# Sorted feed-forward: first eight tiles from the counts of 12 and 15 token tiles

## Chip, cores and metric

The kernel runs on one core of one Trainium2 chip. The metric is the device time of one execution in microseconds; of several executions the median is given.

## What is computed

Two perceiver layers over 64 sequences of 32 latents with 256 features, float32 throughout: 2048 rows, 16 token tiles of 128. Each layer adds a cross-attention, a self-attention and a feed-forward to `x`, each on a layer norm. The change touches the end of the second layer, its self-attention and its feed-forward with one expert of eight for each row:

```python
def _L1_ffn_ref(hidden_states, router_w, gate_w, up_w, down_w):
    H, I, E = (256, 512, 8)
    x = hidden_states.reshape(-1, hidden_shape[-1])
    route = jax.nn.sigmoid(x @ router_w)
    max_ind = jnp.argmax(route, axis=1)
    max_prob = jnp.take_along_axis(route, max_ind[:, None], axis=1)
    out = jnp.zeros_like(x)
    for e in range(num_experts):
        mask = (max_ind == e)[:, None]
        h = jax.nn.silu(x @ gate_w[e]) * (x @ up_w[e])
        out = out + jnp.where(mask, h @ down_w[e], 0.0)
    out = out * max_prob
    return out.reshape(hidden_shape)

x = x + _L1_attn_ref(_layernorm(x, axis=-1), ...)
x = x + _L1_ffn_ref(_layernorm(x, axis=-1), ...)
```

## The kernel before, in words

TensorE (PE) multiplies, VectorE (DVE) and ScalarE (ACT) do the element-wise work, GpSimd (POOL) does some of it and issues the indirect transfers (scatters), and SyncE (SP) issues the other transfers.

**Second self-attention (lines 1556 to 1844).** A loop of slots, `t` from 0 to 16. In slot t TensorE makes the scores of tile t+1 (`score`, line 294), the weighted values of tile t-1 (`gather`, 1627), the values of tile t+1 (1602) and the transposed probabilities of tile t (`heads_on_partitions`, 263). DVE scales the scores and takes their maximum (245, 254), POOL subtracts it (255), ACT takes the exponential (1594). After `gather` DVE divides (1635, 1637) and POOL adds the result to the residual `x` (1640). In the slots before 12 the features of the next group of four tiles are made too (1249), and their norms (`norm`, 205). Weights of one expert matrix after another are loaded by SP in slots 0 to 11 (1519). PE, DVE and ACT keep the order in which the code is written (`manual_schedule`); POOL and SP get theirs from a scheduler.

**Router.** For each group of token tiles: `route_stats` (mean and variance of the finished rows, DVE 161, 162), `route_norm` (reciprocal root on POOL 148, 149; scale and shift on DVE 1657, 1658; normalised rows on ACT 1664; the two numbers kept in the row on POOL 1668), `route_turn` (transposes 1678, copies 1681), `route` (logits 1690, sigmoid from an exponential on ACT 1699, one-hot of the best expert on DVE 1700 to 1708, running counts `cum` 1712), and `send` (rank within the expert by two matmuls 1720 and 1723, slot number on DVE 1727 to 1733, then one scatter a token tile on POOL, 1736). A scatter writes 128 rows of `x`, with probability, token index, scale and shift behind them, to places in a DRAM buffer `srt`, which has a region of 2048 rows for each expert. Groups of four tiles, 0 to 11, take these steps in slots 4g+5, 4g+6, 4g+7 and 4g+8; tiles 12 to 14 and tile 15 take theirs in slots 15, 16 and after the loop.

**Table.** `count` (1746 to 1773) sums the one-hots of all 16 tiles, gets from them how many tiles of 128 rows each expert needs, and makes for the 23 tiles of the sorted feed-forward the first row in `srt` (`rowi`) and the offset of the expert's weights (`tei`).

**Sorted feed-forward (1851 to 1941).** 23 tiles, since eight experts that are each rounded up to whole tiles need at most 16+7. `fetch_rows` loads the rows of a tile by SP (1860), waiting for all scatters (`sent`), normalises them (DVE 1864), keeps the token index `ti` (1868, four buffers) and transposes them (PE 1871, ACT copy 1873). In the loop over j TensorE does the gate product of tile j (1879), the transposes of tile j-1's hidden rows (1891, DVE copy 1893), the up product of tile j, the transposes of tile j+1's rows and the down product of tile j-1 (1899). ACT does Silu (1934), DVE the product with up (1935) and the scaled output with the residual (1907), POOL scatters it to `out` (1910). Only PE keeps a written order here.

Of the kernel before, what the change touches and what calls it, by code (L numbers as in the profile page):

```python
# [45 lines left out]
def perceiver_kernel(ctx: ExitStack, tc: tile.TileContext, a: dict, out: bass.AP):  # L46
# [158 lines left out]
    def norm(g, part, name, mvs, lat):  # L205

        if g >= NG:
            return
        two = range(2 * (part % 2), 2 * (part % 2) + 2)
        if part == 0:  # L210
            mvs[g], lat[g] = sm(f"lnm_{name}{g}", [P, 4, 2]), []
        if part < 2:
            for i in two:
                stats(mvs[g][:, i, :], xs[4 * g + i], f"{name}{g}_{i}")
        else:
            lat[g] += [ln_out(xs[4 * g + i], *mvs[g], i, f"{name}{g}") for i in two]
        if part == 1:
            mvs[g] = ln_scale(mvs[g], f"{name}{g}", power=True)
# [1322 lines left out]
    ntile = numbers("ntile", [[P, NS]], 0, NS)  # L1541
# [6 lines left out]
    nc.vector.memset(cum[:, 0, :], 0.0)  # L1548
    slots = w1.tile([P, NT], mybir.dt.uint32, name="slots")
    for t in range(NT):  # L1550
        nc.gpsimd.tensor_copy(xf[t][:, D : D + 1], token[:, t : t + 1])

# [3 lines left out]
    with tc.tile_pool(name="wE", bufs=2) as work, tc.tile_pool(  # L1556
# [85 lines left out]
        rows = {}  # L1642
        sent = []

        def route_stats(t):
            g, i = divmod(t, 4)
            if i == 0:
                rows[g] = sm(f"lnf_{g}", [P, 4, 2])
            stats(rows[g][:, i, :], xs[t], f"f{t}")

        def route_norm(ts):
            g, i0 = divmod(ts[0], 4)
            n_ = len(ts)
            mv = rows[g][:, i0 : i0 + n_, :]
            sc2 = sm(f"lnq_f{ts[0]}", [P, 4, 2])
            rs = rstd_of(mv, n_, f"f{ts[0]}", True)
            nc.vector.tensor_copy(sc2[:, :n_, 0], rs)
            nc.vector.scalar_tensor_tensor(
                sc2[:, :n_, 1], mv[:, :, 0], -1.0, rs, ALU.mult, ALU.mult
            )  # L1660
            rows[ts] = []
            for i, t in enumerate(ts):
                y = xnp.tile([P, D], F32, tag="xn", name=f"xn_f{t}")
                nc.scalar.activation(
                    y, xs[t], AF.Identity, scale=sc2[:, i, 0:1], bias=sc2[:, i, 1:2]
                )
                rows[ts].append(y)
                nc.gpsimd.tensor_copy(xf[t][:, D + 2 : DP], sc2[:, i, :])

        def route_turn(ts, k):  # L1670
            if k == 0:
                rows[ts] = rows[ts], work.tile(
                    [P, KC, 512], F32, tag="xTf", name=f"xTf{ts[0]}", bufs=1
                )
            xn, xT = rows[ts]
            tp = ps2.tile([P, 512], F32, tag="mm", name=f"tpf{ts[0]}_{k}")
            for i in range(len(ts)):
                nc.tensor.transpose(
                    tp[:, i * P : (i + 1) * P], xn[i][:, k * P : (k + 1) * P], ident
                )  # L1680
            nc.scalar.copy(xT[:, k, : len(ts) * P], tp[:, : len(ts) * P])

        def route(ts):

            n_, t0 = len(ts), ts[0]
            xT = rows.pop(ts)[1]
            l_ps = ps2.tile([P, n_, NE], F32, tag="mm", name=f"lpf{t0}")
            for i in range(n_):
                for k in range(KC):
                    nc.tensor.matmul(  # L1690
                        l_ps[:, i, :],
                        xT[:, k, i * P : (i + 1) * P],
                        f_r[:, k, :],
                        start=(k == 0),
                        stop=(k == KC - 1),
                    )
            rt = sm(f"rtf_{t0}", [P, n_, NE])

            nc.scalar.activation(rt, l_ps, AF.Exp, scale=-1.0)
            nc.vector.tensor_scalar_add(rt, rt, 1.0)  # L1700
            nc.vector.reciprocal(rt, rt)
            mx = sm(f"mxf_{t0}", [P, n_])
            nc.vector.tensor_reduce(mx, rt, AX.X, ALU.max)
            nc.vector.tensor_tensor(rt, rt, bc(mx, 2, NE), ALU.is_equal)
            nc.vector.tensor_tensor(rt, rt, bc(desc[:, 0:NE], 1, n_), ALU.mult)
            m2 = sm(f"m2f_{t0}", [P, n_])
            nc.vector.tensor_reduce(m2, rt, AX.X, ALU.max)
            nc.vector.tensor_tensor(
                oh[:, t0 : t0 + n_, :], rt, bc(m2, 2, NE), ALU.is_equal
            )  # L1710
            for i, t in enumerate(ts):
                nc.vector.tensor_add(cum[:, t + 1, :], cum[:, t, :], oh[:, t, :])
                nc.gpsimd.tensor_copy(xf[t][:, D + 1 : D + 2], mx[:, i : i + 1])

        def send(ts):

            n_ = len(ts)
            gs = slice(ts[0], ts[0] + n_)
            rank = ps2.tile([P, n_ * NE], F32, tag="mm", name=f"rank{ts[0]}")
            nc.tensor.matmul(  # L1720
                rank, tri, oh[:, gs, :].rearrange("p t e -> p (t e)"), start=True, stop=False
            )
            nc.tensor.matmul(
                rank, one, cum[:, gs, :].rearrange("p t e -> p (t e)"), start=False, stop=True
            )
            sl = sm(f"slr_{ts[0]}", [P, n_, NE])
            nc.vector.tensor_tensor(
                sl, rank.rearrange("p (t e) -> p t e", e=NE), bc(base, 1, n_), ALU.add
            )
            nc.vector.tensor_tensor(sl, sl, oh[:, gs, :], ALU.mult)  # L1730
            slf = sm(f"slf_{ts[0]}", [P, n_])
            nc.vector.tensor_reduce(slf, sl, AX.X, ALU.add)
            nc.vector.tensor_copy(slots[:, gs], slf)
            for t in ts:

                d = nc.gpsimd.indirect_dma_start(
                    out=srt,
                    out_offset=bass.IndirectOffsetOnAxis(ap=slots[:, t : t + 1], axis=0),
                    in_=xf[t],
                    in_offset=None,  # L1740
                ).ins
                for e in sent:
                    tc.declare_no_dep(d, e.name, reason="rows of different tokens")
                sent.append(d)

        def count():

            cnt = ps2.tile([P, NE], F32, tag="mm", name="cnt")
            nc.tensor.matmul(cnt, one, cum[:, NT, :], start=True, stop=True)
            n_t = w1.tile([P, NE, NT], F32, name="n_t")  # L1750
            nc.vector.tensor_tensor(n_t, bc(cnt, 2, NT), bc(n128, 1, NE), ALU.is_gt)
            tiles = w1.tile([P, NE], F32, name="tiles")
            nc.vector.tensor_reduce(tiles, n_t, AX.X, ALU.add)
            nc.vector.tensor_scalar_mul(tiles, tiles, float(P))
            last = w1.tile([P, NE], F32, name="last")
            nc.vector.tensor_tensor_scan(last, one[:, 0:NE], tiles, 0.0, ALU.mult, ALU.add)

            L = NE - 1
            te = w1.tile([P, NS, L], F32, name="te")
            nc.vector.tensor_tensor(te, bc(ntile, 2, L), bc(last[:, 0:L], 1, NS), ALU.is_ge)  # L1760
            tef = w1.tile([P, NS], F32, name="tef")
            nc.vector.tensor_reduce(tef, te, AX.X, ALU.add)
            nc.vector.tensor_tensor(te, te, bc(tiles[:, 0:L], 1, NS), ALU.mult)
            row = w1.tile([P, NS], F32, name="row")
            nc.vector.tensor_reduce(row, te, AX.X, ALU.add)
            nc.vector.tensor_sub(row, ntile, row)
            nc.vector.scalar_tensor_tensor(row, tef, float(B * S), row, ALU.mult, ALU.add)
            rowi = w1.tile([P, NS], I32, name="rowi")
            nc.vector.tensor_copy(rowi, row)
            nc.vector.tensor_scalar_mul(tef, tef, float(FE))  # L1770
            tei = w1.tile([P, NS], I32, name="tei")
            nc.vector.tensor_copy(tei, tef)
            return rowi, tei


        routing = {}
        for g in range(3):
            for z, step in enumerate((route_norm, route_turn, route, send)):
                routing[4 * g + 5 + z] = [(step, tuple(range(4 * g, 4 * g + 4)))]
        most, rest = (12, 13, 14), (15,)  # L1780
        routing[15].append((route_norm, most))
        routing[16] += [(route_turn, most), (route_norm, rest)]
        routing[17] = [
            (route, most), (route_turn, rest), (send, most), (route, rest), (send, rest)
        ]

        def router_parts(t):

# [246 lines left out]
```

## Time and profile before

| | us |
|---|---|
| median of 5 runs | 1287.35 (1277.8 to 1293.15) |
| the profiled execution | 1289.4 |
| its span | 1287.6 |
| PE, DVE, ACT, POOL busy | 1186.9, 773.2, 554.5, 367.2 |
| first matmul of the sorted feed-forward | 1143.14 after the span's start |
| last matmul | 1279.75, 1.99 long |

A row of the timeline has start, duration, engine, line, operation, what is written and read, the number of instructions taken together, and in brackets how long the engine had been idle and what ended that. PEld is the weight load of TensorE. A row of busy times by stretch has the stretch, its length, busy time with number of instructions for PE, PEld, DVE, ACT and POOL, the granted TensorE clock as a share of full speed, the mean share of busy transfer engines, and GB/s. DMA_INDIRECT on POOL is a scatter; the duration is POOL's, not the transfer's.

### The profile page before, as it was taken

The page shows a single profiled execution, that of the slowest core. Times are in us where ns is not written, and L with a number is a line of the kernel's source. Part 1 is how long each engine was busy: PE and PEld are TensorE (multiplying, and loading weights), DVE is VectorE, ACT ScalarE, POOL GpSimd, SP SyncE. Part 2 cuts the span into 40 slices and gives each one's busy share as a digit, 9 for nine tenths or more (in the row PEclk, how much of TensorE's full clock was granted, in tenths as well). Part 3 has the DMA queues.
Part 4 walks back from the last instruction along what each step waited for, and adds up shares of the span by engine and source line. Part 5 has one row for each costly group of instructions (what it writes and reads, how often), then busy time and mean ns, then how long its engine had stood idle before and what let it go on. Part 6 is the DMA issues. An engine that isn't in the chain of part 4 may idle for free. (4 is left out here: it accounts for less than half of the span.)

```text
span 1287.6 us, 26074 instructions
## 1 busy us (share of the span) xinstructions
PE 1186.9 (92%) x10173; PEld 831.2 (65%) x10173; DVE 773.2 (60%) x1801; ACT 554.5 (43%) x1297; POOL 367.2 (29%) x438
## 2 busy tenths in 40 slices
PE   7999999999999998999889999999998798669997
PEld 4556767677776565776757766767765566536664
DVE  5676147778768775433297878776774564434343
ACT  2437344464543641213355656565563454311111
POOL 2333334445442621000154252010011354411111
PEclk8889999999999998979989999999999797669999
DMA  5021122333242423902253353111100344011110
GB/s 151 34 69 35 28 75 75 122 117 108 76 140 67 150 74 123 260 4 68 56 159 103 63 149 96 46 36 46 36 1 2 133 150 150 18 38 42 43 40 18
DMA packets 94971, 103.08 MB, mean 80 GB/s; under 512 B 37792, under 2 KB 71329, under 8 KB 94626
## 3 DMA queue, kind: packets, MB, share of 16 engines
q1 hardware_dynamic: 92978, 97.19, 25.7%
q0 software_dynamic: 1872, 4.23, 0.9%
q8 instruction: 81, 1.33, 0.4%
q14 instruction: 40, 0.33, 0.1%
HBM read 69.45 MB, written 32.85 MB: 79 GB/s over the span
## 5 line engine op out<-in xcount | busy, mean ns | idle before, releaser
L1348 ACT ACTIVATE pp<-Sd,nm 128x257 f32<-128x257 f32 x256 | 118.0, 474 | 77.9 <-DVE nm L1344 73.3
L761 PE MATMUL qb<-xT_b,b_q 128*128 128x256 f32 x512 | 123.4, 389 | 0.0
L761 PEld LDWEIGHTS qb<-xT_b,b_q 128*128 128x128 f32 x512 | 96.4, 193 | 39.9 <-issue 19.8
L852 PE MATMUL yb<-b_o,oTb 128*128 128x256 f32 x512 | 115.1, 384 | 0.0
L852 PEld LDWEIGHTS yb<-b_o,oTb 128*128 128x128 f32 x512 | 97.6, 192 | 14.0 <-issue 1.0
L1357 DVE TENSOR_TENSOR pp<-pp,rd 128x514 f32<-128x514 f32 x128 | 102.3, 799 | 2.1
L1344 DVE TENSOR_REDUCE nm<-Sd 128x2 f32<-128x514 f32 x128 | 83.0, 685 | 19.3 <-PE Sd L1336 19.2
L1379 ACT COPY pTd<-pt 128x512 f32<-128x512 f32 x112 | 61.5, 599 | 53.6 <-PE pt L1373 53.6
L1396 PE MATMUL od<-pTd,na 128*64 128x256 f32 x480 | 67.0, 401 | 12.9 <-issue 11.6
L780 POOL TENSOR_TENSOR q2b<-qTb 128x512 f32<-128x512 f32 x64 | 65.5, 1052 | 28.2 <-ACT qTb L769 17.0
L1336 PE MATMUL Sd<-ct,qTd 64*128 64x257 f32 x480 | 68.9, 404 | 0.3 <-ACT pp L1348 0.2
L769 ACT COPY qTb<-qb 128x512 f32<-128x512 f32 x64 | 37.4, 584 | 72.4 <-PE qb L761 70.8
L1373 PE MATMUL pt<-cst,pp 128*128 128x128 f32 x512 | 66.9, 274 | 0.0
L871 POOL TENSOR_TENSOR ynb<-ynb,vec 128x256 f32<-128x256 f32 x16 | 11.6, 724 | 188.3 <-DVE ynb L870 188.3
L1373 PEld LDWEIGHTS pt<-cst,pp 128*128 128x128 f32 x512 | 58.9, 141 | 9.8 <-issue 5.4
L1134 PE MATMUL qd<-xT_d,d_m 128*128 128x256 f32 x256 | 64.4, 395 | 0.2 <-ACT xT_d L230 0.2
L814 DVE RECIPROCAL rqb<-rqb 128x512 f32<-128x512 f32 x16 | 53.5, 3344 | 17.8 <-ACT rqb L809 17.8
L643 PE MATMUL yc<-c,hc 128*128 128x256 f32 x256 | 59.9, 390 | 2.6 <-DVE hc L638 2.6
L1412 PE MATMUL yd<-d_n,co 128*128 128x256 f32 x256 | 62.3, 398 | 0.0
L1910 POOL DMA_INDIRECT out_dram<-os,ti x23 | 22.6, 984 | 126.0 <-DVE os L1907 103.1
L1134 PEld LDWEIGHTS qd<-xT_d,d_m 128*128 128x128 f32 x256 | 46.8, 192 | 17.0 <-issue 6.4
L1412 PEld LDWEIGHTS yd<-d_n,co 128*128 128x128 f32 x256 | 49.3, 198 | 13.1 <-issue 6.5
(371 smaller groups left out, 2381.5 us busy)
## 6 DMA issues: line engine op xcount, KB each, us to landing
srt<-pad SPq DMA_DIRECT2D x17, 1040.0 KB
mb<-maskd SPq DMA_DIRECT2D x64, 128.0 KB
ct<-ctd SPq DMA_DIRECT2D x30, 257.0 KB
rct<-in_ctxT_dram SPq DMA_DIRECT2D x32, 128.5 KB
rrt<-in_ctxT_dram SPq DMA_DIRECT2D x64, 64.2 KB
ctd<-rct SPq DMA_DIRECT2D x32, 128.5 KB
nad<-rna SPq DMA_DIRECT2D x16, 256.0 KB
fw<-in_f_wg_dram SPq DMA_DIRECT2D x8, 512.0 KB
```

What stands on the lines that cost most here:

```text
L761: nc.tensor.matmul(q_ps[:, hh, :], b_q[:, k, h * P : (h + 1) * P], xT[:, k, c0 : c0 + 256], start=(k == 0), stop=(k == KC - 1),)
L780: nc.gpsimd.tensor_tensor(q2[:, 4 * h4 : 4 * h4 + 4, :], q, q, ALU.mult)
L852: nc.tensor.matmul(y_ps, oT[:, h, :], b_o[:, h, :], start=(h == 0), stop=(h == NH - 1))
L1134: nc.tensor.matmul(q_ps[:, r, :], m[:, k, pr * P : (pr + 1) * P], xT[:, k, c0 : c0 + 256], start=(k == 0), stop=(k == KC - 1),)
L1336: nc.tensor.matmul(s_ps[:, hh, :NKV], qT[hs, b % 8, 4 * u : 4 * u + 4, :], ct[hs, b % 4, :], start=True, stop=True,)
L1344: nc.vector.tensor_reduce(nm, s_ps[:, :, :NKV], AX.X, ALU.max, negate=True)
L1348: nc.scalar.activation(pp[:, hh, :], s_ps[:, hh, :NKV], AF.Exp, bias=nm[:, hh : hh + 1], accum_out=sd[:, hh : hh + 1],)
L1357: nc.vector.tensor_tensor(pp, pp, bc(rd, 2, NKV), ALU.mult)
L1373: nc.tensor.transpose(pt[:, hh * 256 + u * P : hh * 256 + u * P + P], probs[b][:, u, hh, c * P : (c + 1) * P], ident,)
L1379: nc.scalar.copy(pT[:, c, :], pt)
L1396: nc.tensor.matmul(o_ps[64 * hh : 64 * hh + 64, 0, :], na[:, j, c, :], pT[:, c, hh * 256 : (hh + 1) * 256], start=(c == 0), stop=(c == 1),)
L1412: nc.tensor.matmul(y_ps, co[:, pr, :], n[:, pr, :], start=(pr == 0), stop=False)
```

## The change

1. `count` becomes `give_out(n_tok, n)`, called three times. After 12 token tiles it gives out 5 tiles, after 15 three more, after 16 the last 15. The first two times it counts only full tiles (`n128e`, whole multiples of 128 rows); what has been given out is kept in `done`, and the later tables begin behind it.
2. The steps of groups 0 to 11 come a slot sooner. `send` is split into `places` (rank and slot number of a group) and `send(t)` (one scatter), and the scatters are spread: one in each of slots 8 to 11, two in slots 12 and 13, four in slot 14.
3. The counts of 12 tiles are taken in slot 15. The first five row loads come right behind the slots, and the router of tiles 12 to 14 and of 15, their scatters, and the second and third table lie between the steps of tiles 0 to 2 of the sorted feed-forward, with logits and counts in the PSUM buffers of tag "y".
4. The sorted feed-forward writes out the order of DVE and ACT too. Row loads are up to five tiles ahead (eight buffers), norms of rows two.
5. In `route_norm` the scale and shift are made by POOL and no longer by DVE; in `norm` the shift is made one part later.

```diff
         else:
+            if part == 2:
+                mv, rs = mvs[g]
+                sh = sm(f"lnh_{name}{g}", [P, 4])
+                nc.vector.scalar_tensor_tensor(sh, mv[:, :, 0], -1.0, rs, ALU.mult, ALU.mult)
+                mvs[g] = rs, sh
...
+    n128e = numbers("n128e", [[P, NT]], 0, NT)
+    nc.vector.tensor_scalar_add(n128e, n128e, float(P - 1))
...
     def route_norm(ts):
...
-            nc.vector.tensor_copy(sc2[:, :n_, 0], rs)
-            nc.vector.scalar_tensor_tensor(
-                sc2[:, :n_, 1], mv[:, :, 0], -1.0, rs, ALU.mult, ALU.mult
-            )
+        nc.gpsimd.tensor_copy(sc2[:, :n_, 0], rs)
+        nc.gpsimd.tensor_tensor(rs, rs, mv[:, :, 0], ALU.mult)
+        nc.gpsimd.tensor_scalar(sc2[:, :n_, 1], rs, -1.0, None, ALU.mult)
...
+    def send(t):
+        nc.vector.tensor_copy(slots[:, t : t + 1], place.pop(t))
+        d = nc.gpsimd.indirect_dma_start(
...
+        for e in sent + loads:
+            tc.declare_no_dep(d, e.name, reason="rows of different tokens")
+        sent.append(d)
+
+    def give_out(n_tok, n, ps, tag):
+        last = n_tok == NT
+        cnt = ps.tile([P, NE], F32, tag=tag, name=f"cnt{n_tok}")
+        nc.tensor.matmul(cnt, one, cum[:, n_tok, :], start=True, stop=True)
+        yield
+        n_t = w1.tile([P, NE, NT], F32, tag="n_t", name=f"n_t{n_tok}")
+        nc.vector.tensor_tensor(
+            n_t, bc(cnt, 2, NT), bc(n128 if last else n128e, 1, NE), ALU.is_gt
+        )
+        left = w1.tile([P, NE], F32, tag="left", name=f"left{n_tok}")
+        nc.vector.tensor_reduce(left, n_t, AX.X, ALU.add)
+        if n_tok > 12:
+            nc.vector.tensor_sub(left, left, done)
...
+        if not last:
+            nc.vector.tensor_scalar(upto, upto, float(n), 0.0, ALU.subtract, ALU.max)
+            nc.vector.tensor_sub(left, left, upto)
+            nc.vector.tensor_scalar_max(left, left, 0.0)
+            nc.vector.tensor_add(done, done, left)
+        yield rowi, tei
...
+            g, z = divmod(t - 5, 4)
+            ts = tuple(range(4 * g, 4 * g + 4))
             fns = []
+            if 0 <= g < 3:
+                if z == 0:
+                    fns += [lambda k=k: route_turn(ts, k, work, ps2, "mm") for k in range(KC)]
+                if z == 1:
+                    fns.append(lambda: route(ts, ps2, "mm"))
+                if z == (1 if g == 2 else 2):
+                    fns.append(lambda: places(ts, ps2, "mm"))
             return fns
+
+        sends = {8: (0,), 9: (1,), 10: (2,), 11: (3,), 12: (4, 5), 13: (6, 7), 14: (8, 9, 10, 11)}
...
+            if t == NT - 1:
+                given = give_out(12, 5, ps2, "mm")
+                parts.append(lambda: next(given))
...
+            if t == NT - 1:
+                table = {0: next(given)}
             if t >= NT - 1:
                 route_stats(t - 1)
+                route_norm(most if t < NT else rest)
...
             if 0 < t < NT - 1:
                 route_stats(t - 1)
+                if t % 4 == 0:
+                    route_norm(tuple(range(t - 4, t)))
+            for t_ in sends.get(t, ()):
+                send(t_)
...
+            for j in range(5):
+                load_rows(j)
+            for k in range(KC):
+                route_turn(most, k, work, ps2, "y")
+            for j in range(2):
+                rows_norm(j)
+            rows_turn(0)
+
+            def router(n_):
+                if n_ == 0:
+                    route(most, ps2, "y")
+                elif n_ == 1:
+                    for k in range(KC):
+                        route_turn(rest, k, work, ps2, "y")
+                elif n_ == 2:
+                    places(most, ps2, "y")
+                    for t in most:
+                        send(t)
+                elif n_ == 3:
+                    given = give_out(15, 3, ps2, "y")
+                    next(given)
+                    table[5] = next(given)
+                    for j in range(5, 8):
+                        load_rows(j)
+                elif n_ == 4:
+                    route(rest, ps2, "y")
+                elif n_ == 5:
+                    places(rest, ps2, "y")
+                    send(rest[0])
+                elif n_ == 6:
+                    given = give_out(NT, NS - 8, ps2, "y")
+                    next(given)
+                    table[8] = next(given)
...
                     g_ps = gate_up(j, 0, rows_of[j][2], off)
+                if j == 0:
+                    router(0)
...
+                router(2 * j + 1)
                 if j + 1 < NS:
-                    rows_of[j + 1] = fetch_rows(j + 1)
+                    rows_turn(j + 1)
                 if j > 0:
                     r, ti, _ = rows_of.pop(j - 1)
                     down(j - 1, r, ti, *made.pop(j - 1))
+                if j < 3:
+                    router(2 * j + 2)
+                if 3 <= j and j + 5 < NS:
+                    load_rows(j + 5)
+                if j + 2 < NS:
+                    rows_norm(j + 2)
```

## The prediction

> **What bounds the kernel now.** I read the page first, then busy time by stages, then the timeline of the stage where TensorE falls idle. On the page TensorE is busy 92% of the span, and its row and the clock row dip together in one place:
>
> ```profile
> PE   7999999999999998999889999999998798669997
> PEclk8889999999999998979989999999999797669999
> ```
>
> Slices 35 and 36 of 40 (1094 to 1159 us, 32.2 us each) have 6 tenths in both. Cut at the events that matter, the end of the last attention product, the first matmul of the sorted feed-forward, and its first full-speed matmul:
>
> ```profile
> 1084.14:1114.25 30.11, 22.66 (x593) 17.75 (x592) 13.75 (x43) 12.67 (x27) 12.82 (x22) 0.73 0.16 55
> 1114.25:1143.14 28.89, 10.29 (x37) 7.64 (x37) 11.40 (x58) 5.43 (x12) 11.92 (x21) 0.50 0.17 55
> 1143.14:1150.44 7.30, 6.84 (x10) 2.78 (x10) 0.86 (x4) 1.12 (x3) 0.00 (x0) 0.59 0.03 8
> 1150.44:1282.30 131.86, 130.52 (x494) 80.95 (x494) 51.08 (x108) 20.95 (x43) 21.65 (x22) 1.00 0.12 36
> ```
>
> The columns are length, busy PE, weight load, DVE, ACT, POOL, granted clock, DMA share, GB/s. From 1150 on TensorE works 130.5 of 131.9 us at full clock: one expert tile per 5.82 us (output scatters at 1168.97, 1174.79, 1180.61). The 28.89 us before it are a latency chain in which no engine is busy even half the time. Its links:
>
> ```profile
> 1113.12 1.13 PE L1627 MATMUL oe<-vde,pT_e 128*32 128x68 f32 x32 [0.28 <-DVE one L1637]
> ...
> 1117.05 1.12 POOL L1736 DMA_INDIRECT srt<-x,slots  x1 [0.54 <-DVE ri_e L1635]
> ...
> 1122.00 0.73 POOL L1640 TENSOR_TENSOR x<-x,one 128x256 f32<-128x256 f32 x1
> ...
> 1124.73 0.60 ACT L1664 ACTIVATE xn_f<-x,lnq_f 128x256 f32<-128x256 f32 x1 [4.53 <-DVE lnq_f L1658]
> ...
> 1136.38 0.18 DVE L1772 CAST tei<-tef 128x23 int32<-128x23 f32 x1
> ...
> 1140.32 0.41 DVE L1864 TENSOR_SCALAR xns<-r 128x256 f32<-128x256 f32 x1 [3.76 <-DMA r<-srt]
> ```
>
> The last tile's residual add stands on POOL behind four scatters (1117.05 to 1122.00); then come its norm, router, places, the table (14 DVE steps, 1133.17 to 1136.56), the row load and at 1143.14 the first gate matmul. The block of four before that (from 1088.61) had stalled DVE in slot 13, and in slot 14 TensorE had waited for normalised rows:
>
> ```profile
> 1094.32 0.43 DVE L161 BATCH_NORM_STATS2 lnb_f<-x 128x6 f32<-128x256 f32 x1 [5.57 <-POOL x L1640]
> ...
> 1100.62 0.14 PEld L1678 LDWEIGHTS tpf<-cst,xn_f 128*128 128x128 f32 x1 [3.21 <-ACT xn_f L1664]
> ```
>
> The end is a fixed tail: last matmul 1281.7, span 1287.6. The profiled execution took 1289.4 us, 1.8 outside its span and 2.05 above the median of 1287.35. I sum against 1289.4 and take the difference over to the median.
>
> **That the tables are valid.** 12 token tiles hold 1536 rows. Eight experts can leave at most 127 rows each outside full tiles, so at least (1536-1016)/128 = 4.06, thus 5, tiles are full; from 15 tiles (1920-1016)/128 = 7.06, thus 8. So five and three tiles always exist, still 23 in all, and the steady stage keeps its 5.82 us a tile. The rival that the change does not do what it says is thereby excluded.
>
> **Where the first gate matmul goes.** I place it by a chain from the start of slot 12 (scores of tile 13, 1084.14), which I hold fixed.
> 1. Slot 12 keeps 3.6 us (to 1087.74). It now holds the norm of tiles 8 to 11. Slot 13 has their transposes, as slot 14 had before, and the same wait for ACT's rows: before that slot took 10.8 us (1096.55 to 1107.38), of which I drop 1.3 for fewer scatters ahead on POOL: 9.5. Slot 14 has scores 1.1, router matmuls 2.2, gather 1.1, rank 1.2 with a wait of 1.0 for the one-hot (as at 1111.66), values 1.9, turn 1.1, all at the half-clock durations of the old slots 14 and 15: 9.6. Sum 22.7: 1106.8.
> 2. The four scatters of tiles 8 to 11 follow on POOL: 1.27 us apart (1117.05, 1118.47, 1119.74, 1121.01), 5.1 us, to 1112. Behind them wait the adds of tiles 14 and 15. The table of 12 tiles, 17 steps at 3.39/14 = 0.24 us, runs on DVE meanwhile (4.1 us) and costs nothing; uncovered it would cost that.
> 3. Add 14 0.73, stats 0.61, norm on POOL 0.24 + 0.88 + three small steps near 0.2, copies 0.44; add 15 0.73, stats 0.61, norm 0.23 + 0.58 + 0.6; ACT row 0.60, two copies 0.48 each, copy of tile 0's rows 0.37. These sum to 8.2; the hops between engines, about 0.1 each, add 0.9: 1121.
> 4. The row load is beside that: last scatter starts at 1111 and lands 2.6 later, the load lands 2.1 after issue (1138.23 to 1140.32), so 1116, while DVE is free for it after stats 15. SP has nothing else queued: the last weight load is issued at 1084.6.
>
> So 1143.1 becomes 1121: **-22.1**. Bounds: POOL's order is not fixed, and if the adds run before the scatters step 3 starts some 5 us sooner and the row load is last (1116 and the 1.4 from landed rows to their copy): 1117; if slot 13 keeps its 10.8 and the sends of two tiles in slots 12 and 13 hold back the softmax as the block of four did (5.57), it is 1128. Between them I take 1121, because the old order put the scatters first.
>
> **What the earlier slots do.** Router steps move one slot forward in slots 4 to 11, same instructions, and the scatters are one to a slot. ACT now waits at the ends of slots 4 and 8 for stats, then POOL's norm (0.24 + 1.05 + 0.6): +2 each at most, since the norm no longer lies a slot behind its stats. DVE no longer stands behind POOL for the shift (1.47 us, twice), and the added small POOL steps lie in an engine busy 38.4 of 79.6 us there (1004.56 to 1084.14). I take 0, bounds -3 and +4.
>
> **What moves into the first tiles.** Per warm rows: 12 router matmuls at 1.95/16 = 0.12, 1.5; two transposes 0.3; two ranks 0.5 each (1057.52 to 1057.99); two counts 0.25 each; four router matmuls 0.5: **+3.8**, all on the path, as TensorE is full. At cold rows the sum is about 7.8 (the 12 took 2.73 at 1120.25). The clock row says which: half speed from 1140 to 1148, 0.86 in the next 4 us, after idleness. If coldness lasts a time, the router's matmuls take the place of cold gate and up matmuls and count warm; if it lasted an amount of work, the 12 would cost 1.2 more. I take time.
>
> The Trainium skill's page "TensorE: Matmul & The Clock Gate", Part 1, puts that time at about 3.4 us; the stretch here is nearer 6, so the figure is not taken over, and by it the 12 matmuls would be warm all the same and the sum unchanged.
>
> **New waits.** DVE and ACT now keep a written order. On DVE, between the products of tiles 1 and 2: product 0.69, table of 15 tiles 20 x 0.24 = 4.8, output 0.48, router of tile 15 1.6 (1129.74 to 1131.34), rows 0.56, hidden copy 0.69, in all 8.8, against 6.6 us of TensorE (5.82 + router). Behind them wait tile 15's rank and tile 1's down product: about 1.3. The last table (16 x 0.24 = 3.9) follows in tile 2: 0.7 more; from tile 3 DVE needs 2.4 of 5.82 us and catches up. **+2.0**, bounds 0 and 5. Tables 2 and 3 are needed for loads of tiles 5 and 8, at least one tile later than they are ready.
>
> ACT gets two more table loads (exponential between two Silu): 1.28 us each in the trace, and the next activation starts at once (load at 382.49, activation at 383.78). ACT has 1 of 5.82 us of work a tile, so they hide; uncovered +2.6.
>
> Against the change speaks the Trainium skill, page "ScalarE: Activation LUTs", What ACT_TABLE_LOAD costs: a switch is 1.28 us plus a drain of 1.38. No row here shows the drain; by the page the uncovered cost would be 5.3, the sum unchanged.
>
> **Sum:** -22.1 + 0 + 3.8 + 2.0 = **-16.3**: 1273.1 for an execution like the profiled one, 1271 as median.
>
> **Rivals.**
> - *POOL lets the residual adds pass the scatters.* First matmul at 1117, -26 + 5.8 = -20, with the bound of the early slots and no DVE wait -25: about 1265. For it: POOL's order is left to a scheduler. Against: at 1117 to 1122 it put the scatters first. 0.17.
> - *The gain is given back.* First matmul at 1128 and 5 us of DVE waits: -15 + 3.8 + 5 = -6, 1281. For it: 5.57 and 3.21 above show how one late POOL queue holds DVE, ACT and TensorE in turn, and DVE is over-full in tile 1. 0.20.
> - *Slower: the written DVE order stands at the token index.* The index of tile j+2 needs the buffer whose scatter left with tile j-2. That scatter lands 3.7 us after its down product (1156.6; issue 1157.84, 2.4 to land); DVE arrives 6.7 us after it, 3.0 to spare. The trace has one such wait, 0.6 us. If scatters landed over 6.7 us late, every tile would wait and hold the next hidden copy; at 1.0 us above that in 21 tiles the sum is +5, at 1.5 +15: 1302. The four late sends on POOL (5.1 us) can do it for two tiles only. 0.07.
>
> **How the numbers follow.** The forecast, -10 to -20, has 0.56. A measurement can tell about 1%, 12.9 us, from no change. Below -12.9 lie 0.45 of the forecast and the first rival: 0.62. Within 1%: 0.11, the second rival, 0.01 of the third: 0.32. Slower by more: 0.06. The range 1260 to 1283 (-27 to -4) leaves out 0.04 of the first rival, 0.06 of the second and the third; the forecast's own is 1267 to 1277.
>
> **What would show it.** Right: first gate matmul near 1121 with scatters just before the add of tile 14; router matmuls between gate and up of tile 0; 23 tiles at 5.82 afterwards; three table loads in the last stage. Wrong: the last attention product later than 1112, gaps of over 2 us on TensorE before tile 3, or a tile longer than 5.9 us after tile 5.

## The result, and the profile after

The change made the kernel a little slower: a median of 1293.38 us (1283.26 to 1302.08, 52 runs) against 1286.79 us before (94 runs), a ratio of 1.0049 with a 95% interval of 1.0037 to 1.0061. Forecast were 1271 us and a range of 1260 to 1283. The profiled execution of the changed kernel took 1289.27 us, next to the 1289.4 of before: two single executions hide a difference of half a per cent, so totals below are medians, and profiles serve for where the time lies.

The page of the changed kernel, TensorE and its clock in 40 slices:

```profile
PE   7999999999999998999989999999998788579997
PEclk8889989999999988989989999999999888669999
```

The dip has not gone. Before it was 6 and 6 in slices 35 and 36; now TensorE has 7, 8, 8, 5, 7 from slice 32 on, and the clock is down in five slices. Busy times by stretch, columns as in the prediction, cut at the start of slot 0 (scores of tile 1), the start of slot 12, the end of the last attention product, the first gate product, and the gates of tiles 1 and 4:

```profile
1003.00:1088.94 85.94, 68.82 (x2038) 49.10 (x2037) 46.92 (x160) 43.32 (x88) 39.47 (x64) 0.88 0.41 139
1088.94:1123.80 34.86, 21.89 (x591) 17.28 (x590) 14.86 (x51) 12.66 (x27) 17.86 (x29) 0.74 0.22 73
1123.80:1135.50 11.70, 2.73 (x8) 1.40 (x9) 5.06 (x25) 3.20 (x7) 4.61 (x16) 0.50 0.24 65
1135.50:1146.67 11.17, 11.17 (x29) 6.82 (x29) 2.57 (x11) 2.92 (x6) 0.44 (x3) 0.50 0.00 0
1146.67:1167.81 21.14, 19.86 (x80) 12.25 (x80) 15.16 (x68) 5.65 (x9) 6.20 (x7) 0.99 0.20 64
1167.81:1281.50 113.69, 112.91 (x429) 69.98 (x427) 43.40 (x95) 18.04 (x37) 19.67 (x20) 1.00 0.11 34
```

The third row is what the change aimed at: 28.89 us before, 11.70 now, 17.2 gained. It was given back ahead of it and behind it. Slots 0 to 11 take 85.94 us (79.58 before: 1084.14 less 1004.56), slots from 12 to the last attention product 34.86 (30.11), and from the first gate to the last product 146.0 (138.6; the last product ends at 1281.54). That is +6.4, +4.8 and +7.4, together 18.6; slot 0 began 1.6 us sooner than before, so that the two profiled executions come out alike. The 6.6 us between the medians do not show in these two.

Rows of the timeline of the changed kernel show the first loss at work, on GpSimd (POOL), ScalarE (ACT) and TensorE in slot 5, and again in slot 13; the last five rows are the end of the attention:

```profile
1031.42 1.04 POOL L149 TENSOR_TENSOR lnr_f<-lnr_f,mhalf 128x4 f32<-128x4 f32 x1
1033.37 2.08 ACT L1586 ACTIVATE xn_f<-x,lnq_f 128x256 f32<-128x256 f32 x4 [1.99 <-POOL lnq_f L1582]
1035.47 0.69 ACT L1262 ACTIVATE qTe<-qe,e_b 128x512 f32<-128x512 f32 x1
1036.21 1.98 PE L1254 MATMUL qe<-xT_e,e_q 128*128 128x512 f32 x4 [3.38 <-ACT qTe L1262]
...
1100.28 2.08 ACT L1586 ACTIVATE xn_f<-x,lnq_f 128x256 f32<-128x256 f32 x4 [3.99 <-POOL lnq_f L1582]
1100.93 1.95 PE L1601 MATMUL tpf<-cst,xn_f 128*128 128x128 f32 x4 [6.80 <-ACT xn_f L1586]
...
1122.18 0.96 POOL L1661 DMA_INDIRECT srt<-x,slots  x1 [0.30 <-issue]
1123.16 0.74 POOL L1810 TENSOR_TENSOR x<-x,one 128x256 f32<-128x256 f32 x1
1126.54 0.42 DVE L161 BATCH_NORM_STATS2 lnb_f<-x 128x6 f32<-128x256 f32 x1
1129.81 0.74 POOL L1810 TENSOR_TENSOR x<-x,one 128x256 f32<-128x256 f32 x1
1135.50 3.75 PE L1935 MATMUL gs<-fw,xTs 128*128 x4 [1.47 <-DMA r<-srt]
```

In slot 5 the first query product ended at 1032.22, and its copy to `qTe` could have followed at once. In ScalarE's written order the four normalised rows of the router stand ahead of it. They wait 1.99 us for GpSimd's norm, then take 2.08; only then comes the copy that frees the one PSUM buffer (PSUM holds TensorE's results), and TensorE has stood for 3.38 us. The Trainium skill, page "TensorE: Matmul & The Clock Gate", Part 1, says that ScalarE's and VectorE's queues are strictly first in, first out; these rows agree: a copy whose input is there waits 3.25 us behind rows written ahead of it, 1.15 until they are ready and 2.1 while they run.

### The profile page after: what moved, and what is told of

Its sections match the earlier page's. It is cut to its first block, busy times and chain, and to the rows that moved or that the text cites. A ratio compares the mean times of both kernels' runs of the same rounds, so it can differ in the third digit from the quotient of the medians.

```text
span 1287.4 us, 26153 instructions
## 1 busy us (share of the span) xinstructions
PE 1188.9 (92%) x10177; PEld 831.1 (65%) x10177; DVE 775.2 (60%) x1845; ACT 556.8 (43%) x1299; POOL 368.5 (29%) x454
## 5 line engine op out<-in xcount | busy, mean ns | idle before, releaser
L785 POOL TENSOR_TENSOR q2b<-qTb 128x512 f32<-128x512 f32 x64 | 65.1, 1045 | 28.2 <-ACT qTb L774 18.5
L1139 PEld LDWEIGHTS qd<-xT_d,d_m 128*128 128x128 f32 x256 | 47.2, 194 | 17.2 <-issue 6.0
L833 DVE RECIPROCAL rdb<-denb 128x512 f32<-128x512 f32 x16 | 53.7, 3355 | 6.8 <-PE denb L831 6.5
L648 PEld LDWEIGHTS yc<-c,hc 128*128 128x128 f32 x256 | 49.4, 195 | 12.1 <-DVE hc L643 3.5
```

Source lines behind the costliest of these rows:

```text
L648: nc.tensor.matmul(y_ps, hs[f][:, i * P : (i + 1) * P], c_2[:, f, :], start=(f == 0), stop=(f == 7),)
L785: nc.gpsimd.tensor_tensor(q2[:, 4 * h4 : 4 * h4 + 4, :], q, q, ALU.mult)
L1139: nc.tensor.matmul(q_ps[:, r, :], m[:, k, pr * P : (pr + 1) * P], xT[:, k, c0 : c0 + 256], start=(k == 0), stop=(k == KC - 1),)
```

## The experiments

Theory A: a norm right behind its statistics stands in ScalarE's written order before GpSimd has made it, and everything queued behind it waits. Rivals for the slots: the single scatters hold GpSimd (B); the transposes share a slot with the query features (C). For the expert stage: the half-speed clock, the table, the written order. (The expectations call A "Theory ACT" and B "Theory scatters"; in that of turns_old "Theory B" is C.) Slots are counted by their starts (scores of tile t+1). Each run had its own comparison with the kernel before, in five rounds:

| run | median us | ratio to before | slots 5-8, 9-12, 13 | last attention product to first gate | first gate to gate of tile 1 |
|---|---|---|---|---|---|
| before | 1286.79 | 1 | 27.4, 29.2, 8.8 | 28.89 | 7.30 |
| the change | 1293.38 | 1.0049 [1.0037, 1.0061] | 32.7, 31.1, 13.7 | 11.70 | 11.17 |
| late_rows | 1283.97 | 0.9969 [0.9943, 0.9995] | 28.8, 31.2, 10.3 | 11.17 | 11.08 |
| sends_moved | 1287.36 | 0.9997 [0.9975, 1.0018] | 34.6, 32.5, 10.9 | 11.07 | 8.45 |
| before_norm_early | 1299.97 | 1.0086 [1.0057, 1.0114] | 31.3, 33.3, 8.3 | 29.74 | 6.76 |
| router_after_up | 1292.30 | 1.0019 [0.9993, 1.0045] | 33.5, 32.6, 13.5 | 12.23 | 10.52 |
| table_sooner | 1292.28 | 1.0030 [0.9999, 1.0061] | 33.6, 32.3, 13.8 | 9.46 | 11.07 |
| warm_gap | 1291.43 | 1.0020 [0.9993, 1.0048] | 33.5, 32.4, 13.7 | 11.15 | 10.61 |
| router_tile_later | 1290.95 | 1.0025 [1.0001, 1.0050] | 33.4, 32.1, 13.9 | 12.20 | 6.86 |
| free_order | 1293.38 | 1.0053 [1.0027, 1.0080] | 32.9, 30.8, 13.3 | 12.26 | 13.23 |
| turns_old | 1294.77 | 1.0023 [0.9989, 1.0057] | 31.1, 33.5, 13.0 | 11.57 | 11.17 |
| old_slots | 1278.14 | 0.9908 [0.9872, 0.9944] | 26.1, 24.9, 14.8 | 12.04 | 11.17 |
| best2 | 1278.91 | 0.9908 [0.9872, 0.9945] | 30.3, 28.2, 7.7 | 9.44 | 6.61 |
| best3 | 1274.30 | 0.9899 [0.9860, 0.9938] | 26.1, 24.9, 11.7 | 9.44 | 6.70 |

Code that no edit touched shows how far single profiles differ. Slots 5 to 12 are the same in the change and in router_after_up, table_sooner, warm_gap, router_tile_later and free_order: 63.7 to 66.1 us. The first expert tile is the same in seven runs: 10.6 to 11.2 us in six, 8.45 in sends_moved.

**The rows of the norm later, and the norm early in the old kernel.** late_rows is the changed kernel with ScalarE's rows (`route_rows`, split off `route_norm`) written just ahead of the first transposes that read them:

```diff
-        rows[ts] = []
+        rows[ts] = sc2
+
+    def route_rows(ts):
+        sc2, rows[ts] = rows[ts], []
...
+                    fns.append(lambda: (route_rows(ts), route_turn(ts, 0, work, ps2, "mm")))
```

> The changed kernel, but ACT's normalised rows of groups 0 to 11 are written into ACT's order only just before their first transposes, one slot later, and in slot 13 those transposes stand behind the gather and the values. Theory ACT (the rows at the ends of slots 4, 8 and 12 stand in ACT's fixed order behind stats and POOL's norm, and hold up the features' copies and the next slot): slots 5, 9 and 13, which lasted 11.6, 12.9 and 13.7 us after and 7.1, 8.4 and 8.8 before, fall back to at most 8.5, 9.5 and 10.5, the first gate matmul comes 8 to 12 us sooner after the scores of tile 1 than the changed kernel's 132.5, and the time falls by 0.6 to 0.9% below the changed kernel (ratio to before about 0.996). Theory scatters (single scatters in POOL's queue hold up POOL's norm and softmax): slots 9 and 13 stay within 1 us of 12.9 and 13.7, the time does not move.

before_norm_early does the reverse to the kernel before: POOL makes scale and shift, and the norms of groups 0 to 11 stand behind their statistics.

```diff
-                if step is route_norm:
+                if step is route_norm and ts[0] >= 12:
...
                 route_stats(t - 1)
+                if t % 4 == 0:
+                    route_norm(tuple(range(t - 4, t)))
```

> The kernel before with two parts of the change alone: scale and shift of the router's norm made by POOL, and the norm of groups 0 to 11 written directly behind the stats of its last tile, at the ends of slots 4, 8 and 12 instead of 5, 9 and 13. Transposes, router, places, scatters and feed-forward as before. Theory ACT: slots 5 and 9 grow by about 4 us each, since the features' copies wait behind the rows; slot 13 by less, as it has no features here and its transposes come a slot later; 0.6 to 0.9% slower than before. Theory scatters: within 0.2% of before.

Both medians moved as theory A says: 0.8% less than the change, and 0.9% more than before. The slots fit less well. In before_norm_early slots 5 and 9 grew by 5.8 and 8.6 us, where about 4 each was expected; in late_rows slots 5, 9 and 13 took 9.9, 13.0 and 10.3 us, where at most 8.5, 9.5 and 10.5 was expected (for slot 9 that is theory B's figure). In the old kernel the wait in slot 9 is larger, since its block of four scatters stands ahead of the norm on GpSimd in slot 9 (timeline of before_norm_early):

```profile
1073.34 2.07 ACT L1663 ACTIVATE xn_f<-x,lnq_f 128x256 f32<-128x256 f32 x4 [6.72 <-POOL lnq_f L1659]
1075.44 0.69 ACT L1257 ACTIVATE qTe<-qe,e_b 128x512 f32<-128x512 f32 x1
```

In late_rows the copy goes first again (timeline, slot 5), but the rows now pace the transposes next to them, and slots 5 to 12 keep 60.0 us of 63.8:

```profile
1035.13 0.69 ACT L1262 ACTIVATE qTe<-qe,e_b 128x512 f32<-128x512 f32 x1 [2.07 <-PE qe L1254]
1035.72 2.06 ACT L1591 ACTIVATE xn_f<-x,lnq_f 128x256 f32<-128x256 f32 x4
```

In slot 9 the copy no longer waits for the rows either, but TensorE's first four query products take 3.51 us there, against 1.98 at the full clock; why the clock was low is not shown. The first gate came 8.55 us sooner behind slot 0 than in the change (8 to 12 expected).

**Scatters out of the slots with a norm** (the changed kernel otherwise):

```diff
-        sends = {8: (0,), 9: (1,), 10: (2,), 11: (3,), 12: (4, 5), 13: (6, 7), 14: (8, 9, 10, 11)}
+        sends = {7: (0, 1), 9: (2, 3), 11: (4, 5), 13: (6, 7), 14: (8, 9, 10, 11)}
```

> The changed kernel with the scatters of tiles 0 to 7 two each at the ends of slots 7, 9, 11 and 13, none in slots 8 and 12, where the norms are. Theory ACT: slot 5 is unchanged (11.6), slots 9 and 13 lose at most the scatters inside the norm's chain, 1.2 of 12.9 and 2.3 of 13.7 us; the time falls by 0.1 to 0.3%. Theory scatters: slots 9 and 13 fall back to about 8.4 and 8.8 us, together 9 us, 0.7%.

The median fell by half a per cent against the change. Slots 5 to 8 and 9 to 12 did not shrink: slot 9, which B wanted at 8.4 us, took 14.6, though no scatter was left in its norm's chain and ScalarE's wait was down to 1.41 us. Slot 13 did shrink, by 2.9 us to 10.9; the two scatters that had lain inside its norm's chain are what theory A allowed for (2.3), while B wanted 8.8.

**Norm, turns, router and ranks of tiles 0 to 7 back in their old slots,** with the spread scatters, the early table and the whole expert stage of the change:

```diff
+            if t in (5, 9):
+                route_norm(tuple(range(t - 5, t - 1)))
...
-                if t % 4 == 0:
+                if t == 12:
                     route_norm(tuple(range(t - 4, t)))
...
-            g, z = divmod(t - 5, 4)
+            g, z = divmod(t - 5, 4) if t > 12 else divmod(t - 6, 4)
```

> The changed kernel with the norm, the turns, the router and the ranks of token tiles 0 to 7 back at the places that they had before the change (norm in the middle of slots 5 and 9 behind the values, turns in 6 and 10, and so on); tiles 8 to 11, the one or two scatters to a slot, and the whole end are those of the change. Theory (a norm behind its statistics holds ScalarE's written order, and the turns share a slot with the query features): slots 5 to 8 fall from 32.7 us to 27 to 28.5, slots 9 to 12 from 31.1 to 29 to 30, the stretch from the first score product to the last attention product from 120.8 to 113 to 116 us, and the median by 4 to 7 us against the changed kernel, to a ratio of 0.999 to 1.002 to the kernel before. Rival (the single scatters in slots 8 to 13 hold GpSimd, and so the adds): slots 5 to 12 stay within 2 us of the changed kernel's sum of 63.8, and the median within 2 us.

Faster than expected: slots 5 to 12 take 51.0 us, 12.9 less than in the change and 5.6 less than before. B falls for these slots: the single scatters are there, and the slots are shorter than in either kernel.

**Only the norm early.** turns_old has the last hunk of that diff alone, so it differs from old_slots in the place of two norms.

> The changed kernel with the turns, the router and the ranks of token tiles 0 to 7 in the slots that they had before the change, but with their norms where the change put them, behind the statistics at the ends of slots 4 and 8. Against the run in which the norms too were put back (slots 5 to 12 together 51.0 us, the changed kernel 63.8), only the place of the norm differs. Theory A (the norm's place is most of the loss: ScalarE's rows wait in their order for GpSimd): slots 5 to 12 take 58 to 62 us and the ratio to the kernel before is 0.997 to 1.003. Theory B (the transposes' sharing a slot with the query features is most of it): slots 5 to 12 take 51 to 55 us and the ratio is 0.990 to 0.994.

64.6 us in slots 5 to 12, 13.7 above old_slots, and a ratio 1.2% above: theory A, and more than it asked; beside early norms the early turns add nothing (63.8 with them), so C falls as the cause of this loss. (Early turns with late rows were run only in late_rows and best2, 60.0 and 58.5 us; there they may cost.) Slot 9 of turns_old, GpSimd, ScalarE and TensorE of the timeline:

```profile
1068.35 0.23 POOL L148 TENSOR_SCALAR lnr_f<-lnf 128x4 f32<-128x4 f32 x1 [0.77 <-DVE slots L1658]
1069.26 1.24 POOL L1661 DMA_INDIRECT srt<-x,slots  x1 [0.69 <-POOL lnr_f L148]
1070.53 1.06 POOL L149 TENSOR_TENSOR lnr_f<-lnr_f,mhalf 128x4 f32<-128x4 f32 x1
...
1072.50 2.07 ACT L1586 ACTIVATE xn_f<-x,lnq_f 128x256 f32<-128x256 f32 x4 [3.32 <-POOL lnq_f L1582]
1074.60 0.69 ACT L1262 ACTIVATE qTe<-qe,e_b 128x512 f32<-128x512 f32 x1
...
1075.34 3.78 PE L1254 MATMUL qe<-xT_e,e_q 128*128 128x512 f32 x4 [5.03 <-ACT qTe L1262]
```

The same slot by stretch, in turns_old and then in old_slots:

```profile
1066.94:1081.78 14.84, 9.81 (x173) 5.41 (x173) 3.91 (x16) 6.16 (x12) 6.06 (x13) 0.77 0.24 82
```

```profile
1058.06:1065.13 7.07, 6.90 (x173) 3.87 (x172) 3.68 (x15) 3.61 (x7) 5.29 (x13) 1.00 0.56 178
```

The scheduler put a scatter between two steps of the norm, so ScalarE waited 3.32 us (1.99 in slot 5 of the change, with no scatter there) and TensorE 5.03 (0.17 in old_slots, where the rows stand later in the slot): 4.9 of the 7.8 us. The other 2.9 are TensorE's own work: busy time rises from 6.90 to 9.81 us with the same 173 instructions, at a granted clock of 0.77 instead of 1.00. The idleness is paid twice.

**The end: the table one slot sooner.**

```diff
-            if t == NT - 1:
+            if t == NT - 2:
                 given = give_out(12, 5, ps2, "mm")
...
                 send(t_)
+            if t == NT - 2:
+                table = {0: next(given)}
```

> The changed kernel with its table of 12 token tiles (counts matmul and 4.1 us of VectorE) written one slot sooner: the matmul behind the ranks of tiles 8 to 11, the table behind the index copies of the four scatters, where VectorE would otherwise wait for GpSimd. Theory (the table is not hidden: in the changed kernel it runs 1122.4 to 1126.6 in front of the statistics of tile 14, and the row loads wait for the last add behind it): the stretch from the last attention product to the first gate product falls from 11.7 us to 7.5 to 8.5, the attention before it stays within 1 us, and the median falls by 3 to 4 us against the changed kernel (0.3%). Rival (the table is hidden and GpSimd sets the end): the stretch stays within 1 us of 11.7. Second rival (given back): the stretch falls, but the last two attention slots grow by as much.

The stretch fell to 9.46 us, 2.2 less, not the 3 to 4 expected; the attention ahead of it took 121.5 instead of 120.8. TensorE now waits 4.02 us for the rows of tiles 12 to 14 where it had waited 6.25 (timeline of the change, then of table_sooner):

```profile
1130.05 2.10 PE L1601 MATMUL tpf<-cst,xn_f 128*128 128x128 f32 x6 [6.25 <-ACT xn_f L1586]
1134.03 2.10 PE L1601 MATMUL tpf<-cst,xn_f 128*128 128x128 f32 x6 [4.02 <-ACT xn_f L1586]
```

The three runs with the early table have 9.44 to 9.46 us there, the nine other runs of the changed kernel 11.07 to 12.26. So in the change the table was hidden only in part. The median (0.2% less) cannot show two microseconds by itself.

**The first expert tile and the clock.** Four runs of the changed kernel. router_after_up and router_tile_later move the router's steps, warm_gap adds products, free_order drops the written order of DVE and ACT.

```diff
-                if j == 0:
+                if j == 1:
                     router(0)
...
-                router(2 * j + 1)
+                if j > 0:
+                    router(2 * j - 1)
...
```

That is router_tile_later; in router_after_up `router(0)` stands behind the up product of tile 0.

> The changed kernel with the 12 router matmuls of tiles 12 to 14 behind the up product of tile 0 and not between gate and up. If coldness of TensorE lasts a fixed time or amount of work, the stretch from the first gate matmul to tile 1's gate matmul stays at 11.2 us (all at half clock). If the narrow router matmuls (8 columns each) keep the clock from rising, the clock rises during or right after the up product, and the stretch falls to 8 to 9.5 us, 0.15 to 0.25% of the time.

> The changed kernel with every router step of the expert stage one tile later: the 12 narrow router products stand between gate and up of tile 1, so that tile 0 holds only its own products. Theory (the router work was run at half clock, and it held the clock down): the first tile falls from 11.17 us to 5.8 to 7.5, the tile with the 12 router products takes at most 7.5 us at the full clock, the stretch from the first gate to the last product falls from 146.0 to 142 to 143.5, and the median by 2.5 to 4 us. Rival (the clock comes back a fixed time after the first gate): tile 0 about 7.3, tile 1 at half clock 9 or more, the stretch within 1 us of 146.

```diff
+            if t == NT:
+                for w_ in range(2):
+                    dm = ps2.tile([P, 512], F32, tag="mm", name=f"dm{w_}")
+                    for k in range(2):
+                        nc.tensor.matmul(dm, ident, fw[:, 0:512], start=(k == 0), stop=(k == 1))
```

> The changed kernel with four additional products of 128x512 (identity by weights, their result is not used) behind the last attention product, where TensorE is idle for about 7 us. Theory (the granted clock falls to 0.50 because TensorE has little work around the end of the attention, and comes back once it has been busy): the first tile, 11.17 us from its gate to the next in the changed kernel, takes 7 to 8.5 us, the first gate is at most 1 us later, and the median falls by 2 to 4 us against the changed kernel. Rival (the clock comes back only after wide products with nothing narrow between them, or at a time of its own): the first tile stays at 10.5 to 11.5 us and the median within 1 us.

```diff
-            engines={
-                mybir.EngineType.PE,
-                mybir.EngineType.DVE,
-                mybir.EngineType.Activation,
-            }
+            engines={mybir.EngineType.PE}
```

> The changed kernel with only TensorE's order written out in the expert stage, as before the change; VectorE and ScalarE are ordered by the scheduler. Theory (the written order costs next to nothing there): first gate within 1 us, the stretch from first gate to last product within 1.5 us of 146.0, the median within 0.2%. Rival (the written order holds VectorE behind the router's chain, the prediction's 2 us): the stretch falls to 143 to 145 us, and the stalls of TensorE in tiles 2 to 5 are gone. Other rival (the scheduler puts the table in front of the row work): slower by 3 us or more.

The first tile by stretch in router_after_up, then in router_tile_later, then the added products and the first tile of warm_gap, then the first tile of free_order:

```profile
1141.39:1151.91 10.52, 8.71 (x28) 4.73 (x29) 2.58 (x12) 2.67 (x6) 0.44 (x3) 0.76 0.00 0
```

```profile
1138.06:1144.92 6.86, 6.40 (x10) 2.62 (x10) 0.57 (x1) 1.71 (x4) 0.00 (x0) 0.63 0.00 0
```

```profile
1131.92:1137.41 5.49, 5.43 (x12) 1.86 (x8) 3.25 (x12) 0.35 (x1) 3.73 (x10) 0.73 0.14 50
1143.15:1153.76 10.61, 10.39 (x28) 6.15 (x29) 2.71 (x12) 2.78 (x6) 0.44 (x3) 0.58 0.01 2
```

```profile
1134.58:1147.81 13.23, 10.70 (x28) 6.39 (x29) 2.96 (x14) 4.57 (x8) 0.44 (x3) 0.63 0.00 0
```

In the change the clock stayed at 0.50 through all 11.17 us. With the router behind the up product the clock came up sooner (0.76 on the mean), but TensorE then stood idle for 1.8 us of the tile, most of it ahead of the ranks, and the tile came out only 0.65 us shorter, between the two expectations. One tile later both were cured: tile 0 takes 6.86 us, and the stretch from first gate to last product falls from 146.0 to 144.3, less than the 142 to 143.5 expected, since the router's 12 products now lengthen tile 1 (8.55 us). The added products did raise the clock, but it fell again in the idle microseconds before the first gate, and the first tile stayed cold for 8.9 of its 10.6 us: filling a gap helps only up to the work that should be warm. Without the written order the stretch grows to 148.7 us: the scheduler leaves TensorE 2.5 us idle in tile 0. The written order is not a cost here.

**Edits together.** best2 has late_rows, sends_moved, router_tile_later and table_sooner; best3 has old_slots, the late rows for tiles 8 to 11, router_tile_later and table_sooner.

> The changed kernel with four edits together: ScalarE's rows of the norms just ahead of the first transposes that read them, the scatters out of the slots with a norm, the expert stage's router steps one tile later, and the table of 12 tiles one slot sooner. By the single runs against the changed kernel (0.8%, 0.5%, 0.2% and 0.2% less) at most 1.7% less, some of it counted twice: a ratio to the kernel before of 0.988 to 0.995, with the first gate 118 to 121 us behind the start of the first score product (132.5 in the changed kernel, 138.6 before). Rival (GpSimd's queue, not ScalarE's, sets the end): no better than the 0.997 of the late rows alone.

> The changed kernel with tiles 0 to 7 normed, turned and routed in the slots of the kernel before, ScalarE's rows of tiles 8 to 11 just ahead of their transposes, the router steps one tile later, and the table one slot sooner. Theory of ScalarE's order and of the shared slot: slots 5 to 12 take 56 to 59 us (56.5 before, 63.8 with the change), the first gate stands 114 to 119 us behind the first score product, and the ratio to the kernel before is 0.984 to 0.992, better than with the late rows in the new slots. Rival (the excess of the slots has another cause): slots 5 to 12 at 61 us or more, and a ratio of 0.993 or more.

best3 by stretch: slots 0 to the last attention product, the chain, tile 0, the rest.

```profile
1005.39:1111.44 106.05, 84.73 (x2627) 62.80 (x2626) 64.56 (x224) 55.86 (x115) 57.05 (x93) 0.87 0.42 136
1111.44:1120.88 9.44, 2.73 (x9) 1.40 (x9) 2.73 (x10) 3.94 (x8) 4.99 (x16) 0.50 0.28 85
1120.88:1127.58 6.70, 6.24 (x10) 2.62 (x10) 0.57 (x1) 1.55 (x4) 0.00 (x0) 0.65 0.00 0
1127.58:1265.00 137.42, 134.93 (x524) 84.22 (x524) 60.24 (x174) 26.81 (x51) 26.06 (x30) 1.00 0.13 38
```

best3 beats both kernels: 1% faster than before and 1.5% than the change. That it is better than best2 or old_slots is not shown; the three intervals overlap.

## Why the prediction was wrong

The gain that it was built on is there: the chain behind the last attention product fell from 28.89 to 11.70 us. What it set at next to nothing beside that took it back. In the two profiles slots 0 to 11 came to +6.4 where 0 was taken, slot 12 to the first gate to -12.4 (59.0 to 46.6 us) where -22.1 was taken, and the first gate to the last product to +7.4 where +5.8 was taken. The miss of 9.7 in the middle is 4.2 in slot 13, 3.4 behind the last scatter and 2.1 in slot 12 and between slot 14 and that scatter, which stays unexplained. One mechanism, priced wrongly, stands behind the losses in slots 5, 9 and 13.

1. **"What the earlier slots do ... +2 each at most ... I take 0, bounds -3 and +4".** This is the failed step. It named the wait (ScalarE at the ends of slots 4 and 8 for GpSimd's norm) but priced it as the length of the wait and set it against small gains elsewhere. It did not name what is queued behind the waiting rows, the copy that frees TensorE's only buffer for the query features, nor that the clock falls after such a gap. Measured, by turns_old against old_slots: +13.7 us for two norms, 4.8 in slot 5, 7.8 in slot 9, 1.1 elsewhere. With the norms back, slots 5 to 12 show a gain of 5.6 us that the forecast had not counted either. Most of it, 3.5, lies in slot 11, where TensorE does the same products at half clock before (8.36 us, the 16 router products 3.58 of them) and at full clock in old_slots (4.88 and 1.95); whether the spread scatters brought that about was not tried.
2. **Item 1 of the chain, "slot 13 has their transposes ... the same wait for ACT's rows ... 9.5".** 13.7 measured, 14.8 in old_slots. Two scatters lay inside the norm's chain, and TensorE waited 6.80 us for ScalarE. Writing these rows just ahead of their transposes took 3 us off (11.7 in best3, 10.3 in late_rows), and so did moving the two scatters (10.9 in sends_moved), so the same cause is at work. Slot 14 and the last products came later too: the last attention product at 34.9 us behind the start of slot 12, where the prediction's own limit was 1112, that is 27.9.
3. **Items 2 and 3, from the last scatter to the first gate, 9 us (1112 to 1121).** 12.4: the last scatter ends at 1123.14, ahead of the last adds as forecast, and the gate comes at 1135.50. The table that "costs nothing; uncovered it would cost" 4.1 stands on VectorE ahead of the statistics of tile 14 (1126.54, while its add on GpSimd was done at 1123.90), and 2.2 us of it were on the path by table_sooner. (The prediction counts 14 steps in the old table, the profile has 13; its price of 4.1 us held, 1122.43 to 1126.63 is 4.2.)
4. **"If coldness lasts a time, ... I take time".** The mis-sized term of the expert stage: tile 0 took 11.17 us, all of it at half clock, 3.9 more than before, where the 12 narrow products, two transposed blocks and the ranks in it had been priced warm at some 2.3 us. The whole stretch of the expert stage grew by 7.4 instead of 5.8 us; with the router in a warm tile it grew by 5.7 (144.3 less 138.6), and the 12 products took 1.40 us where 1.5 was priced, so the warm price itself was right.
5. **New waits, +2.0.** 1.3 us: the stretch of tiles 1 to 3 has 21.14 us with 19.86 busy. (The prediction's own 8.8 against 6.6 us would be 2.2 for tile 1, not the 1.3 that it wrote.) At the token index TensorE waited once, 0.62 us. The two additional table loads of ScalarE were hidden, as forecast. Of the rivals, "the gain is given back" came nearest, and its sentence that a late GpSimd queue holds "DVE, ACT and TensorE in turn" is the mechanism; its price of +7 on the first gate was too low.

best3 shows what the idea was worth without the failed steps: 1274.3 against 1289.9 us, -15.6 (forecast -16.3). That is luck in part and no proof of the terms, since two misses cancel in it: the slots 0 to 11 gained 6.9 us (forecast 0), and the way from slot 12 to the first gate took 42.8 us (forecast 36.9).

## What to carry to other kernels

Where an engine keeps a written order, an operation may be moved earlier only as far as its input is ready by then; price it by what is queued behind it and who waits for that, not by its own wait. An engine that seems half idle can still be the one that a full engine waits for. Work put into the first tile after an idle stretch is paid at the clock that the idleness left, so put narrow products a tile later.

## What the runs showed of the hardware

The half-speed stretch behind an idle chain was not of one length. From the first gate product to the rise of the granted clock, worked out from the mean clock of the first tile (between 0.50 and 1.00), it was 6.0 us before the change, 5.1 in router_after_up and router_tile_later and 4.7 in best3, all with wide products alone up to there. With the 12 products of 8 columns from about 3.5 us on, it was 8.9 in warm_gap, 9.3 in late_rows and table_sooner, and over 11.17 in the change, old_slots and turns_old, though TensorE was busy nearly all of that time (9.8 in free_order, with 2.5 us idle); only in sends_moved had the clock risen (after 3.9 us) as they began, and there the 12 took 1.56 us instead of 2.57. So narrow products that begin before the clock is up seem to hold it down; whether by their narrowness or by the pauses among them was not tried apart. The Trainium skill, page "TensorE: Matmul & The Clock Gate", Part 1, gives about 3.4 us of sustained work, counted in a free-running window, whatever is issued; wide products here needed 3.9 to 6.0, a spread that a window running by itself leaves room for; the runs with narrow ones don't agree with it.

In warm_gap the clock rose about 4.0 us after TensorE had become busy, and was back at 0.50 by 1142, some 2.4 us after the router's transposes that followed them had ended, with 0.4 us of work in between. Pauses of 3.38 and 5.03 us inside the attention went with a mean clock of 0.86 and 0.77 in their slots (turns_old, slots 5 and 9).
